# The bias product of a GraphSAGE layer over 128 rows instead of three, in a fused attention and GraphSAGE kernel

## The chip, the core and the metric

The kernel runs on one core of one Trainium2 chip. The metric is device time of one execution in microseconds (us); the table below gives the median of three runs. Times with a decimal point that follow an instruction's name are starts counted from the first instruction of one profiled execution.

## What is computed

The input is a batch of 16 graphs of 1024 nodes with 128 features each, and a weighted adjacency of 1024 x 1024 per graph. Layer 0 is an eight-headed attention that is masked and weighted by the adjacency. Layer 1 first thins the adjacency row by row ("dilation"), and then runs three GraphSAGE steps on the thinned one; in the reference, cut to what matters:

```python
def _sage(x, adj, Wr, Wx, b, mf):
    deg = jnp.clip(jnp.sum(adj, axis=-1, keepdims=True), 1.0, None)
    agg = jnp.einsum('bij,bjd->bid', adj, x) / deg
    out = agg @ Wr + x @ Wx + b
    nrm = jnp.maximum(jnp.linalg.norm(out, axis=-1, keepdims=True), NORM_EPS)
    return out / nrm * mf[..., None]
...
h1 = _bn(jax.nn.relu(_sage(x, adj_d, Wr1, Wx1, b1, mf)), g1, be1)
h2 = _bn(jax.nn.relu(_sage(h1, adj_d, Wr2, Wx2, b2, mf)), g2, be2)
h3 = _bn(jax.nn.relu(_sage(h2, adj_d, Wr3, Wx3, b3, mf)), g3, be3)
xc = jnp.concatenate([h1, h2, h3], axis=-1) * mf[..., None]
return (xc @ Wl + bl) * mf[..., None]
```

The change concerns the `+ b` in `_sage`. `_bn` needs the mean and variance over all graphs, so the three steps can't overlap: each ends in a short stretch in which the statistics are finished before the next begins.

## The kernel before

The program is one long unrolled list of instructions. TensorE (PE), VectorE (DVE) and ScalarE (ACT) run it in the order in which the Python code issues it (`manual_schedule`, L1186); the order was written out by hand, with generators that are advanced at fixed places. SP's queue and GpSimd's queue issue the transfers.

**First part, to about 2414 us.** Attention over all 256 pieces of the adjacency, with the dilation beside it. TensorE works here mostly in parts of its array: 32 rows (score products, L545 and L551) or 32 columns (sums of values, L478 and L483).

**GraphSAGE, from 2414.6 to about 3487 us.** Three steps L = 0, 1, 2, sixteen graphs b, two halves c of 512 nodes: 96 turns in the order L, b, c. A turn is one call of `nodes` (L1081), interleaved with the end of the turn before it and with work for the next graph. On TensorE a turn issues in this order:

- the bias product (`start_with`, L111), which opens the accumulator `own` and lays the bias under all 512 columns. The fp32 bias was cut into three bf16 pieces at the start (`biases`, L90); the product of a 3 x 128 matrix of ones with the 3 x 512 pieces adds them up again, the 128 columns of the piece repeated four times;
- the node's own product x @ Wx into the same accumulator (L1092, four products; every fp32 product is two instructions in the trace, so eight);
- the sums over neighbours `pg` (L1106), four groups of 16 instructions. After the second group comes the transposition `pt` of the **previous** turn's result (L1143, four instructions), except in the first turn of a step. Between the groups stand products for the next graph (`given`, L1077; in step 0 the transposes L1060) and, in the turns of the second half (c = 1) of steps 1 and 2, the output products `py` of the step before (L1033).

On VectorE, once the sums of a turn are complete, there runs in fixed order: scaling and adding (L1124, four), one piece of the next turn's masking (L145, the thinning of the adjacency, four pieces a turn), the row sums of squares (L1132, after ScalarE's L1129), L1134, another piece of L145, L1137, L1138, and L1139, which makes the result `o`. TensorE's `pt` (L1143) reads `o`. In step 0 the degrees (L1117, L1120) come first. Then follow two more pieces of L145 and the statistics L1150. In the turns with c = 1 of steps 1 and 2, VectorE also adds up the output products (L1038).

So turn n's sums release a stretch of VectorE work, and turn n+1's TensorE list waits for the end of it at `pt`, halfway. The bias product of turn n+1 stands between the two.

The bias product is also used in attention, in `value` (L322) and at the end of `conclude` (L413), 32 times each. The constants are made at the very start: `ones3` (L83, L84) by VectorE; `bias3` (L88) is filled by three small transfers on GpSimd's queue (L105).

The adjacency for the turns is fetched by `edges` (L128) on SP's queue, three to four turns ahead.

Of the kernel before, what the change touches and what calls it, by code (L numbers as in the profile page):

```python
# [11 lines left out]
BF = mybir.dt.bfloat16  # L12
# [9 lines left out]
P = 128  # L22
# [12 lines left out]
def swept(ctx: ExitStack, tc: tile.TileContext, t: dict, out: bass.AP, flag: bass.AP):  # L35
# [8 lines left out]
    nc = tc.nc  # L44
    x, adj, nodemask = t["x"], t["adj"], t["nodemask"]
    B, N, D = x.shape
# [6 lines left out]
    const = ctx.enter_context(tc.tile_pool(name="const", bufs=1))  # L53
# [26 lines left out]

        return ap.unsqueeze(2).to_broadcast([P, ap.shape[-1], d])

    ones3 = const.tile([3, P], BF, name="ones3")  # L83
    nc.vector.memset(ones3, 1.0)  # L84


    names = ["L0_gnn_bv", "L0_gnn_bo"] + [f"L1_gnn_b{i + 1}" for i in range(3)]
    bias3 = const.tile([3, len(names), D], BF, name="bias3")  # L88

    def biases():  # L90
        n = len(names)
# [13 lines left out]
            nc.gpsimd.dma_start(bias3[i : i + 1], pieces[i])  # L105
        yield

    def start_with(ps_tile, pieces):

        n = ps_tile.shape[1]  # L110
        nc.tensor.matmul(  # L111
            ps_tile.rearrange("p k d -> p (k d)"), ones3, pieces.unsqueeze(1).to_broadcast([3, n, D]),
            start=True, stop=False,
        )

# [50 lines left out]
    def first_part(p1):  # L166
# [32 lines left out]
        names = ("Wk", "Wv", "Wq", "Wo")  # L199
# [8 lines left out]
        own = one.tile([P, 2], F32, name="own")  # L208
# [75 lines left out]
        def prepare(b):  # L284


            yield False
            xt = xts.pop(b)
            h = shared.tile([P, NB, D], F32, name=f"h_{b}", tag="s", bufs=2)
            hT = shared.tile([P, N], F32, name=f"hT_{b}", tag="s", bufs=2)  # L290

            def turned(c, bank=(ps_m, "m")):
                pt = bank[0].tile([P, 512], F32, name=f"pt_{b}_{c}", tag=bank[1])
                for i in range(HB):
                    nc.tensor.transpose(pt[:, i * P : (i + 1) * P], h[:, c * HB + i, :], ident)
                yield "evict"
                nc.scalar.copy(hT[:, c * HN : (c + 1) * HN], pt[:, :HN])


            kT = pool.tile([P, N], F32, name=f"kT_{b}", tag="kT")  # L300

            def query(c, bank=(ps_m, "m")):
                pq = bank[0].tile([P, 512], F32, name=f"pq_{b}_{c}", tag=bank[1])
                nc.tensor.matmul(pq, wts["Wq"], hT[:, c * HN : (c + 1) * HN], start=True, stop=True)
                yield "evict"
                for g in range(2):
                    nc.scalar.activation(  # L307
                        qTs[c][:, g, :], pq, AF.Identity, bias=bq[:, g : g + 1], scale=own[:, g : g + 1]
                    )

            def key(c, bank=(ps_m, "m")):
                cc = slice(c * HN, (c + 1) * HN)
                pk = bank[0].tile([P, 512], F32, name=f"pk_{b}_{c}", tag=bank[1])
                nc.tensor.matmul(pk, wts["Wk"], hT[:, cc], start=True, stop=True)
                yield "evict"
                nc.scalar.activation(kT[:, cc], pk, AF.Identity, bias=bk)

            v1 = v1s[b % 2]

            def value(c, bank=(ps_m, "m")):  # L320
                pv = bank[0].tile([P, HB, D], F32, name=f"pv_{b}_{c}", tag=bank[1])
                start_with(pv, bias3[:, 0, :])  # L322
                for i in range(HB):
                    n = (c * HB + i) * P
                    nc.tensor.matmul(
                        pv[:, i, :], hT[:, n : n + P], wts["Wv"], start=False, stop=(i == HB - 1)
                    )
                yield "evict"
                nc.scalar.copy(
                    v1[:, c * HB : (c + 1) * HB, :, :HD], pv.rearrange("p k (h d) -> p k h d", d=HD)  # L330
                )

            if b == 0:

                first = layer_norm_relu(h, xt, "a0", 0, HB)
                for _ in range(2):
                    next(first)
                yield "weights"
                yield from first
                yield "weights"  # L340
                yield "biases"
                yield from turned(0)
                yield "turn 1"
                second = layer_norm_relu(h, xt, "a0", HB, NB)
                for _ in range(2):
                    next(second)
                yield from key(0)
                qTs = [pool.tile([P, 2, HN], F32, name=f"qT_{b}_0", tag="qT")]
                yield from query(0, (ps_d, "d"))
                yield from second  # L350
                ready[b] = (xt, qTs, kT, v1)
                yield True
                yield from value(0, (ps_d, "d"))
                yield True
                yield from turned(1)
            else:
                yield from layer_norm_relu(h, xt, f"a{b}")
                for c in range(2):
                    yield True
                    yield from turned(c)  # L360
                for what in (key, value):
                    yield True
                    yield from what(0)

                yield "half 1"
                qTs = [pool.tile([P, 2, HN], F32, name=f"qT_{b}_0", tag="qT")]
                yield True
                yield from query(0)

            ready[b] = (xt, qTs, kT, v1)  # L370
            for what in (key, value):
                yield True
                yield from what(1)
            yield "half 0"
            qTs.append(pool.tile([P, 2, HN], F32, name=f"qT_{b}_1", tag="qT"))
            yield True
            yield from query(1)

        def conclude(b, c, acc, xt):

            yield False
            cx = small.tile([P, HB, H, HD], F32, name=f"cx_{b}_{c}", tag="cx", bufs=1)
            oTs = []
            for g in range(2):
                oT = small.tile([P, HN], F32, name=f"oT_{b}_{c}_{g}", tag="oT", bufs=2)
                nc.scalar.copy(oT, acc[g])
                oTs.append(oT)
            for g in range(2):
                yield True
                on = ps_m.tile([P, HB, 4, 32], F32, name=f"on_{b}_{c}_{g}", tag="m")  # L390
                for i in range(HB):
                    nc.tensor.transpose(
                        on[:, i, :, :].rearrange("p h d -> p (h d)"), oTs[g][:, i * P : (i + 1) * P], ident
                    )
                yield "evict by VectorE"
                rd = small.tile([P, HB, 4], F32, name=f"rd_{b}_{c}_{g}", tag="rd", bufs=2)
                nc.vector.reciprocal(rd.unsqueeze(3), on[:, :, :, HD : HD + 1])
                nc.vector.tensor_tensor(
                    cx[:, :, g::2, :], on[:, :, :, :HD], rd.unsqueeze(3).to_broadcast([P, HB, 4, HD]), ALU.mult
                )  # L400
                nc.gpsimd.tensor_copy(rden[:, 2 * b + c, :, 4 * g : 4 * g + 4], rd)
            yield True
            pc = ps_m.tile([P, 512], F32, name=f"pc_{b}_{c}", tag="m")
            for i in range(HB):
                nc.tensor.transpose(
                    pc[:, i * P : (i + 1) * P], cx[:, i, :, :].rearrange("p h d -> p (h d)"), ident
                )
            yield "evict"
            cxT = small.tile([P, HN], F32, name=f"cxT_{b}_{c}", tag="oT", bufs=2)
            nc.scalar.copy(cxT, pc)  # L410
            yield True
            pr = ps_m.tile([P, HB, D], F32, name=f"pr_{b}_{c}", tag="m")
            start_with(pr, bias3[:, 1, :])  # L413
            for i in range(HB):
                nc.tensor.matmul(
                    pr[:, i, :], cxT[:, i * P : (i + 1) * P], wts["Wo"], start=False, stop=(i == HB - 1)
                )
            yield "evict by VectorE"
            part = xt[:, c * HB : (c + 1) * HB, :]
            nc.vector.tensor_tensor(part, part, pr, ALU.add)  # L420
            if c == 1:
                yield False
                nc.sync.dma_start(x1_d[b], xt)
                yield from layer_norm_relu(xt, xt, f"b{b}")
                nc.sync.dma_start(h0_d[b], xt)
# [655 lines left out]
    def nodes(L, b, c, hT, aT):  # L1081
# [4 lines left out]
        k0 = b * NB + c * HB  # L1086
        width = D + 1 if L == 0 else D
        own = bank(f"own_{L}_{b}_{c}", "o").rearrange("p (k d) -> p k d", d=D)
        start_with(own, bias3[:, 2 + L, :])
        for i in range(HB):  # L1090
            n = (c * HB + i) * P
            nc.tensor.matmul(own[:, i, :], hT[:, n : n + P], wts[f"Wx{L + 1}"], start=False, stop=(i == HB - 1))  # L1092
# [93 lines left out]
    with tc.manual_schedule(  # L1186
# [6 lines left out]
        for L in range(3):  # L1193
# [10 lines left out]
            for b in range(B):  # L1204
# [4 lines left out]
                for c in range(2):  # L1209
                    i = (L * B + b) * 2 + c  # L1210
# [738 lines left out]
```

## Time and profile before

| | us |
|---|---|
| median of 3 runs | 3541.1 (3537.39 to 3546.47) |
| profiled execution, first to last instruction (the only time that the profile gives of it) | 3538.5 |
| TensorE busy (34855 matmuls) | 3433.7, 97% |
| VectorE busy | 3172.6, 90% |
| ScalarE busy | 2289.3, 65% |
| GraphSAGE: bias product of the first turn of steps 0, 1, 2 | 2414.6, 2767.6, 3132.1 |
| a c = 0 turn and the c = 1 turn after it, step 2 | 10.47 and 11.67 |

How to read it: the profile has one row per instruction, with a start and a duration. TensorE's matmuls are pipelined and their ends are modelled, so a row's duration is no measure of what the instruction costs: the distance from one start to the next is. A row such as `PE L1106 MATMUL pg<-y,aT 128*128 128x128 f32 x16` says that 16 instructions used 128 rows and 128 columns of the array and wrote 128 x 128 fp32 each; `3*128` is three rows and 128 columns. `PEld` are the loads of the stationary operand. The bracket at the end of a timeline row is the engine's idle time before it and what ended it.

### The profile page before, as it was taken

What the parts mean: (1) busy time and instruction counts of PE and PEld (TensorE: products, weight loads), DVE (VectorE), ACT (ScalarE), POOL (GpSimd) and SP (SyncE); (2) the same over time, 40 slices, a digit from 0 to 9 for tenths busy, and PEclk for the clock granted to TensorE, in tenths of its full rate; (3) what the DMA queues carried; (4) which work ended last, traced back from release to release, by engine and by line L of the source; (5) the groups of instructions that cost most, each with busy time, mean ns of one, the idle gap of its engine ahead of it and who ended that gap; (6) DMA issues with size and microseconds to landing.
All of it is one profiled execution on the core that took longest, in us unless ns stands there. A gap on an engine that the chain in (4) does not pass through costs nothing. (4 is left out here: it accounts for less than half of the span.)

```text
span 3538.5 us, 86073 instructions
## 1 busy us (share of the span) xinstructions
PE 3433.7 (97%) x34855; PEld 1884.6 (53%) x34855; DVE 3172.6 (90%) x5254; ACT 2289.3 (65%) x3781; POOL 177.6 (5%) x253
## 2 busy tenths in 40 slices
PE   8999999999999999999999999999999899999997
PEld 2333333333333333333333333337999899989997
DVE  7999999999989999999999999997878788878886
ACT  7699689679769869968876885873222333322224
POOL 2000000000000000000000000000000000000000
PEclk9999999999999999999999999999999999999999
DMA  7356456447537636735753873677999799889996
GB/s 233 103 173 195 126 157 195 143 132 221 171 110 216 201 115 198 223 117 163 232 170 118 243 213 108 191 228 263 331 328 331 274 328 331 325 308 333 332 333 217
DMA packets 650121, 772.27 MB, mean 218 GB/s; under 512 B 173264, under 2 KB 569168, under 8 KB 637424
## 3 DMA queue, kind: packets, MB, share of 16 engines
q1 hardware_dynamic: 632672, 708.58, 62.1%
q0 software_dynamic: 15456, 57.30, 4.9%
q8 instruction: 275, 4.51, 0.5%
q14 instruction: 134, 1.10, 0.1%
q10 hardware_dynamic: 1584, 0.79, 0.1%
HBM read 508.50 MB, written 157.29 MB: 188 GB/s over the span
## 5 line engine op out<-in xcount | busy, mean ns | idle before, releaser
L594 DVE TENSOR_TENSOR w<-e,aT 128x1024 f32<-128x1024 f32 x1024 | 1203.7, 1217 | 98.0 <-ACT e L589 97.6
L589 ACT ACTIVATE e<-sc 128x1024 f32<-128x1024 f32 x1024 | 990.8, 1020 | 373.8 <-PE sc L551 369.5
L1106 PE MATMUL pg<-y,aT 128*128 128x128 f32 (+1 forms) x6144 | 737.3, 275 | 0.0
L1106 PEld LDWEIGHTS pg<-y,aT 128*128 128x128 f32 x6144 | 711.8, 192 | 0.0
L478 PE MATMUL acc<-w,v_both 128*32 128x512 f32 x4096 | 676.7, 606 | 10.9 <-DVE w L594 5.7
L483 PE MATMUL acc<-e,eps 128*32 128x512 f32 x4096 | 653.3, 594 | 0.0
L551 PE MATMUL sc<-qT,kT 32*128 32x512 f32 x4096 | 584.0, 640 | 0.3 <-ACT qT L307 0.3
L145 DVE SCALAR_TENSOR_TENSOR aT<-mr,aT 128x1024 f32<-128x1024 bf16 x384 | 458.7, 1216 | 0.0
L483 PEld LDWEIGHTS acc<-e,eps 128*32 128x32 f32 x4096 | 165.5, 110 | 295.0 <-issue 284.9
L1129 ACT ACTIVATE sq<-o 128x512 f32<-128x512 f32 x96 | 60.6, 631 | 361.6 <-DVE o L1124 361.6
L882 DVE TENSOR_TENSOR_SCAN wr<-rk 128x1024 f16<-128x1024 bf16 x128 | 291.6, 2278 | 0.0
L545 PEld LDWEIGHTS <-never 32*32 32x32 bf16 x8192 | 78.2, 87 | 340.1 <-issue 318.5
L545 PE MATMUL sc<-nomask,never 32*32 32x512 bf16 x8192 | 247.0, 385 | 10.8 <-ACT e L589 7.5
L478 PEld LDWEIGHTS acc<-w,v_both 128*32 128x32 f32 x4096 | 106.9, 108 | 241.0 <-DVE w L594 148.9
L551 PEld LDWEIGHTS sc<-qT,kT 32*128 32x128 f32 x4096 | 160.0, 183 | 116.9 <-issue 116.1
L496 PEld LDWEIGHTS pa<-ident,a 128*128 128x128 f32 x1024 | 107.8, 141 | 181.2 <-issue 136.5
L1147 ACT COPY hT<-pt 128x512 f32<-128x512 f32 x96 | 56.3, 586 | 224.2 <-PE pt L1143 214.3
L1124 DVE SCALAR_TENSOR_TENSOR o<-pg,rdeg,mine 128x128 f32<-128x128 f32 x384 | 108.1, 344 | 88.9 <-PE pg L1106 87.1
L895 ACT ACTIVATE wr<-wr,th 128x1024 f16<-128x1024 f16 x128 | 148.0, 1156 | 46.5 <-DVE wr L882 45.6
L496 PE MATMUL pa<-ident,a 128*128 128x128 f32 x1024 | 168.5, 287 | 6.5 <-DMA a<-in_adj 5.8
L503 ACT ACTIVATE nomask<-aT 128x512 bf16<-128x512 f32 x256 | 161.4, 630 | 8.1
L499 ACT COPY aT<-pa 128x512 f32<-128x512 f32 x256 | 151.5, 592 | 12.0 <-PE pa L496 6.2
(225 smaller groups left out, 3927.5 us busy)
## 6 DMA issues: line engine op xcount, KB each, us to landing
aT<-aT_d SPq DMA_DIRECT2D x94, 2048.0 KB, 8.9
mr<-mr_d SPq DMA_DIRECT2D x188, 512.0 KB, 5.8
aT_d<-aT SPq DMA_DIRECT2D x256, 256.0 KB, 4.2
a<-in_adj SPq DMA_DIRECT2D x253, 256.0 KB, 4.2
ad<-in_adj SPq DMA_DIRECT2D x112, 512.0 KB, 4.3
nomask<-nomask SPq DMA_DIRECT2D x512, 96.0 KB, 2.7
nomask<-nomask SPq DMA_DIRECT2D x512, 64.0 KB, 2.6
nomask<-nomask SPq DMA_DIRECT2D x512, 32.0 KB, 2.8
```

Of the source, the lines that this page charges most:

```text
L145: nc.vector.scalar_tensor_tensor(part, mrs[h][:, j : j + 2, :].rearrange("p j n -> p (j n)"), 0.0, part, ALU.is_equal, ALU.mult)
L478: nc.tensor.matmul(acc[g][32 * j : 32 * j + 32, :], v1[:, m, 2 * j + g, :], ws[j // 2][:, j % 2, :], start=(m == 0), stop=False,)
L483: nc.tensor.matmul(acc[g][32 * j : 32 * j + 32, :], eps8, es[j // 2][:, j % 2, :], start=False, stop=(m == NB - 1),)
L496: nc.tensor.transpose(pa[:, k * P : (k + 1) * P], a[:, k, :], ident)
L499: nc.scalar.copy(aT[:, 0, :], pa)
L503: nc.scalar.activation(nomask[:, 0, :], aT[:, 0, :], AF.Relu, bias=1.0, scale=-1e38, accum_out=zeros[:, i : i + 1])
L545: nc.tensor.matmul(scs[j // 2][to : to + 32, j % 2, :], never[rows, rows], nomask[rows, j, :], start=True, stop=False, tile_position=(32 * ...
L551: nc.tensor.matmul(scs[j // 2][:, j % 2, :], kT[rows, mm], qTs[c][rows, g, :], start=False, stop=True, tile_position=(32 * j, 0),)
L589: nc.scalar.activation(e, scs[q], AF.Exp, scale=1.0 / math.sqrt(HD))
L594: nc.vector.tensor_tensor(w, es[q], aT.to_broadcast([P, 2, HN]), ALU.mult)
L882: nc.vector.tensor_tensor_scan(wrs[b], rk(b, 1, N + 1), rk(b, 2, N + 2), -1023.0, ALU.add, ALU.add)
L1106: nc.tensor.matmul(pg[:, i // 2, at : at + width], aT[:, j, i * P : (i + 1) * P], y[:, j, :width], start=(j == 0), stop=(j == NB - 1),)
```

## The change

`ones3` becomes a 128 x 128 matrix of ones, and `bias3` gets 128 rows, of which the last 125 are zero. The bias product of GraphSAGE takes all 128 rows; those of attention take the first three rows of the same tiles, as before. The set of products, their order, their output and the sums that they give are the same. New is one memset of the 128 x 640 bf16 tile on VectorE at the start, which the three transfers into that tile then have to follow.

```diff
-    ones3 = const.tile([3, P], BF, name="ones3")
-    nc.vector.memset(ones3, 1.0)
+    ones_bf = const.tile([P, P], BF, name="ones_bf")
+    nc.vector.memset(ones_bf, 1.0)
...
-    bias3 = const.tile([3, len(names), D], BF, name="bias3")
+    bias3 = const.tile([P, len(names), D], BF, name="bias3")
+    nc.vector.memset(bias3, 0.0)
...
-    def start_with(ps_tile, pieces):
+    def start_with(ps_tile, i, rows=3):
 
         n = ps_tile.shape[1]
         nc.tensor.matmul(
-            ps_tile.rearrange("p k d -> p (k d)"), ones3, pieces.unsqueeze(1).to_broadcast([3, n, D]),
+            ps_tile.rearrange("p k d -> p (k d)"), ones_bf[:rows], bias3[:rows, i, :].unsqueeze(1).to_broadcast([rows, n, D]),
             start=True, stop=False,
         )
...
-                start_with(pv, bias3[:, 0, :])
+                start_with(pv, 0)
...
-            start_with(pr, bias3[:, 1, :])
+            start_with(pr, 1)
...
-        start_with(own, bias3[:, 2 + L, :])
+        start_with(own, 2 + L, P)
```

## The prediction

> **What bounds the kernel now.** I read the page first, then TensorE's timeline over two turns of GraphSAGE, then VectorE's over the same turns, then the waits step by step. From the page: over the span TensorE is the fullest engine, and in GraphSAGE (the last quarter of the slices) the DMA engines are busy too.
>
> ```profile
> PE 3433.7 (97%) x34855; PEld 1884.6 (53%) x34855; DVE 3172.6 (90%) x5254; ACT 2289.3 (65%) x3781; POOL 177.6 (5%) x253
> DMA  7356456447537636735753873677999799889996
> ```
>
> That alone would say: shorten TensorE's list and the time follows. The timeline of TensorE over a c = 0 turn and the c = 1 turn after it (step 2) says otherwise:
>
> ```profile
> 3374.64 0.39 PE L111 MATMUL own<-bias,ones 3*128 3x512 bf16 x1
> 3374.96 1.16 PE L1092 MATMUL own<-weights,h 128*128 128x128 f32 x8
> 3375.95 3.74 PE L1106 MATMUL pg<-y,aT 128*128 128x128 f32 x32
> 3380.08 0.63 PE L1143 MATMUL pt<-ident,o 128*128 128x128 f32 x4 [0.39 <-DVE o L1139]
> ...
> 3383.23 1.95 PE L1106 MATMUL pg<-y,aT 128*128 128x128 f32 x16
> 3385.11 0.38 PE L111 MATMUL own<-bias,ones 3*128 3x512 bf16 x1
> 3385.43 1.16 PE L1092 MATMUL own<-weights,h 128*128 128x128 f32 x8
> 3386.42 1.06 PE L1077 MATMUL pn<-weights,h 128*128 128x128 f32 x8
> ...
> 3391.78 0.60 PE L1143 MATMUL pt<-ident,o 128*128 128x128 f32 x4
> ```
>
> In the first turn TensorE stands before `pt`: 32 instructions of `pg` at 0.112 us end their issue at 3375.95 + 3.58 = 3379.53, and `pt` starts at 3380.08. In the second there is no wait. VectorE shows why; what releases it is the end of the sums before the bias product:
>
> ```profile
> 3374.75 1.12 DVE L1124 SCALAR_TENSOR_TENSOR o<-pg,rdeg,mine 128x128 f32<-128x128 f32 x4 [0.66 <-PE pg L1106]
> 3379.25 0.69 DVE L1139 SCALAR_TENSOR_TENSOR o<-o,f 128x512 f32<-128x512 f32 x1
> ...
> 3389.72 0.69 DVE L1139 SCALAR_TENSOR_TENSOR o<-o,f 128x512 f32<-128x512 f32 x1
> ```
>
> From 3374.75 to 3379.94 VectorE works without a pause, 5.2 us from the end of the old sums to `o`; `pt` follows 0.15 later. Bias product, L1092 and half of the sums are TensorE's share beside it, and in a c = 0 turn of steps 1 and 2 that share is the shorter one. In a c = 1 turn, which also holds `pn` and `py`, `o` is ready at 3390.41 and TensorE gets there at 3391.78: 1.37 us to spare. So c = 0 turns are paced by VectorE up to `pt`, c = 1 turns by TensorE. The waits of TensorE (us in total, times, longest), taken over step 0, step 1 and step 2, agree:
>
> ```profile
> PE pt L1143 <- DVE o L1139: 6.6, 4, 4.7
> ...
> PE pt L1143 <- DVE o L1139: 12.2, 17, 2.5
> ...
> PE pt L1143 <- DVE o L1139: 6.0, 15, 0.4
> ```
>
> Step 0 has only four long ones, but there `pt` is late too, by a gap too short for that list. TensorE's and then VectorE's rows:
>
> ```profile
> 2593.95 0.66 PE L1143 MATMUL pt<-ident,o 128*128 128x128 f32 x4
> 2594.45 1.95 PE L1106 MATMUL pg<-y,aT 128*128 128x129 f32 x16
> ...
> 2588.29 0.16 DVE L1117 TENSOR_SCALAR rdeg<-pg 128x4 f32<-128x4 f32 x1 [1.44 <-PE pg L1106]
> 2593.21 0.69 DVE L1139 SCALAR_TENSOR_TENSOR o<-o,f 128x512 f32<-128x512 f32 x1
> ```
>
> `o` ends at 2593.90 and `pt` starts 0.05 after, its four instructions taking 0.50 to the next row, where an unhindered set (3391.78 to the `pg` at 3392.22) takes 0.44. It holds in both halves: `o` ends 0.05 to 0.07 before `pt` from turn 2 to turn 28. Step 0 is balanced with VectorE just ahead in the say.
>
> [...] the trace has no 128-row bf16 product of 512 columns, but eight bf16 transposes of 128 columns (L889) take 56 ns each, so at most 224 for 512. [...] The trace's loads read 91 ns for the three-row ones and 192 for fp32.
>
> **The change, part by part.** *The product itself.* Before, from starts: a block of 16 `pg` ahead of it takes 1.88 to the bias (3383.23 to 3385.11) where a block followed by an fp32 row takes 1.79 (3392.22 to `py` at 3394.00): 0.09 too much. Bias to L1092: 0.31. L1092 then takes 0.99 (3385.43 to 3386.42) where eight fp32 rows, `pn`, take 0.89 (3386.42 to `pg` at 3387.31): 0.10 too much[...]. After, with one array shape: no excess before, 0.22 for the product with the load of L1092's weights beside it, no excess after. Saved: 0.09 + (0.31 - 0.22) + 0.10 = 0.29, call it **0.30** with the 0.213 that a half-speed stretch suggests for the product (below). That fp32 and bf16 follow one another in one shape without loss is not shown at 128 rows; at 32 rows it is: in attention the bias product (1011.40) follows the last of L551's fp32 rows after 0.41[...] and only its exit, to 128 rows, costs: 0.31 to L415 (1011.71). Bounds: 0.18 [...] (0.09 + 0.09), 0.31 at most; below nothing only by the third rival.
>
> *Where it lies on the path.* The saved time lies between the end of the sums and `pt`.
> - c = 1 turns of step 1: 15 of 16 (the last has no next graph and waits). The margin before `pt`, from the end of L1139 in each to TensorE's arrival, is 1.37, in the last of them 0.48: more than 0.30. 15 x 0.30 = 4.5.
> - c = 1 turns of step 2: all 16, margins 1.37, 0.48 and 0.64 in the last two. 16 x 0.30 = 4.8.
> - The first turn of steps 1 and 2 has no `pt`; after its bias product `pg` follows without a wait. Step 2: 0.30. Step 1 runs at half clock there (bias 2767.58, L1092 2768.11, 0.53 apart, of which 0.427 would be the product, twice 0.213): 0.4.
> - The first turn of step 0 comes from the 32-column shape, so the entry stays: 0.2, and TensorE's list leads from there to the check of the attention (PE to L420 to L973).
> - All c = 0 turns of steps 1 and 2 and all later turns of step 0: **nothing**. TensorE reaches `pt` 0.30 earlier and waits 0.30 longer; in c = 0 turns the idle row grows from 0.39 to about 0.7. Late next is still `o`.
>
> Sum: 4.5 + 4.8 + 0.3 + 0.4 + 0.2 = **10.2 us** of the 28.8 that 96 x 0.30 would be.
>
> *What follows from earlier turns.* A pair of turns in step 2 lasts 22.14, the DMA engines being busy 0.91 of it; at 21.84 it is 0.92, and no wait of TensorE, VectorE or ScalarE in GraphSAGE is for a DMA. In the c = 1 turns VectorE has 0.77 us idle before L1038 and 0.66 before the next L1124, both behind TensorE, so it follows.
>
> *The start.* The new memset has 640 columns; by the fp32 ones (128 columns 0.165, 1024 columns 0.912) it takes 0.6 at most. VectorE is idle for 1.19 us before it casts the identity (2.35), and the memset fits there: nothing; 0.6 if that cover were gone. It is far ahead of the transfers into that tile, which wait for VectorE's pieces until 11.03. The ones tile takes 0.165 for three or for 128 rows. Attention's 64 bias products keep their three rows and cost what they did.
>
> The profiled execution has a span of 3538.5, so 3528.3 after; it lies 2.6 under the median of 3541.1 and within its runs. From the median: 3541.1 - 10.2 = **3531**.
>
> **The rivals.**
> - *Every turn pays.* If the 0.30 were on the path in all 96 turns: 3541.1 - 28.8 = 3512. For it: TensorE is busy 97%. Against it: the rows of `o` and `pt` above, in two turns of three.
> - [...] If the excess comes from the 512-column bf16 product among fp32 ones, or what is won is handed back to the transfers (busy 0.91, so with 0.09 in reserve against a shortening of 0.014), the time stays at 3541. For it: no 128-row pair of this kind in the trace. Against it: the free entry at 32 rows.
> - *Slower.* At 128 rows the ones load like fp32 weights, 0.1 in the open, while both ends stay as they are. Then the path turns lose 0.1 each, 34 x 0.1 = 3.4: 3544.5; c = 0 turns of step 2 have a wait of 0.55 before `pt` that swallows it, step 0 has none, and with its 28 turns it is 3547. It decides from the point where the stretch from last `pg` to second row of L1092 is longer than now (0.21 + 0.31 + 0.21 = 0.73). [...]
>
> **How the numbers follow.** Forecast 0.80, every turn 0.05, no change 0.11, slower 0.04. With 0.18 to 0.31 for the saving the forecast's own times are 3534.7 to 3530.5, and runs spread by some 4 us to either side (3537.4 to 3546.5 before), so 3524 to 3540 holds about eight in ten; it leaves out the first rival and most of the third. About 0.3%, 10.6 us, is what a measurement of this kernel can tell from no change, and 10.2 is just under it: I give faster 0.45 (the forecast on its good side, and the first rival), same 0.52, slower 0.03.
>
> **What would show it.** Right: the bias row reads 128*128 and L1092 starts 0.21 to 0.22 after it, eight L1092 rows take 0.89, c = 1 turns of step 2 last 11.37, c = 0 turns still 10.47 with a longer wait for `o`, and step 0 lasts as long as before. Wrong: c = 0 turns get shorter (first rival), the distances round the bias row stay (second) or grow (third), or a wait for a DMA appears.

## The result, and the profile after

| | before | after |
|---|---|---|
| median (lowest to highest), us | 3540.89 (3537.39 to 3546.47), 8 runs | 3532.36 (3524.36 to 3538.27), 8 runs |
| ratio, with its 95% interval | | 0.9972 (0.9961 to 0.9982) |
| profiled execution, first to last instruction | 3538.5 | 3533.7 |
| c = 0 and c = 1 turn, step 0 | 10.82 and 9.93 | 10.82 and 9.92 |
| c = 0 and c = 1 turn, step 1 | 10.71 and 11.67 | 10.71 and 11.37 |
| c = 0 and c = 1 turn, step 2 | 10.47 and 11.67 | 10.47 and 11.37 |

The turns are medians over turns 2 to 27 of each step (counted from 0), in us from one bias product to the next. The ratio is worth 9.9 us (6.4 to 13.8); 10.2 had been forecast, and 3531 for the time.

The line numbers of the changed kernel, and of those made from it, are one higher than before: the bias product is L112, the node's own product L1093, `pg` L1107, `o` L1140, `pt` L1144.

The page after, in the two lines that were read before:

```profile
PE 3411.2 (97%) x34855; PEld 1887.4 (53%) x34855; DVE 3172.5 (90%) x5255; ACT 2290.3 (65%) x3781; POOL 177.7 (5%) x253
DMA  7356456447537636745753773677999799989996
```

TensorE is busy 22.5 us less, and VectorE has one instruction more, the memset. The span is 4.8 shorter. So most of what TensorE's list lost is not in the span, and these lines don't say where it went. TensorE's timeline over the same two turns of step 2 does (start, duration, instruction, idle time before it):

```profile
3349.13 0.38 PE L112 MATMUL own<-bias,ones_bf 128*128 128x512 bf16 x1
3349.34 1.05 PE L1093 MATMUL own<-weights,h 128*128 128x128 f32 x8
3350.23 3.74 PE L1107 MATMUL pg<-y,aT 128*128 128x128 f32 x32
3354.67 0.63 PE L1144 MATMUL pt<-ident,o 128*128 128x128 f32 x4 [0.70 <-DVE o L1140]
...
3357.81 1.95 PE L1107 MATMUL pg<-y,aT 128*128 128x128 f32 x16
3359.60 0.38 PE L112 MATMUL own<-bias,ones_bf 128*128 128x512 bf16 x1
3359.81 1.05 PE L1093 MATMUL own<-weights,h 128*128 128x128 f32 x8
3360.70 1.06 PE L1078 MATMUL pn<-weights,h 128*128 128x128 f32 x8
...
3366.06 0.60 PE L1144 MATMUL pt<-ident,o 128*128 128x128 f32 x4
...
3370.97 0.38 PE L112 MATMUL own<-bias,ones_bf 128*128 128x512 bf16 x1
```

Three distances have changed: a block of 16 `pg` to the bias is 1.79 (3357.81 to 3359.60), bias to L1093 is 0.21, and eight L1093 rows take 0.89 (3359.81 to 3360.70). The c = 1 turn is 3370.97 - 3359.60 = 11.37. In the c = 0 turn `pt` stands behind an idle 0.70 where it was 0.39, and the turn is 10.47 as before. VectorE over the same turns:

```profile
3349.33 1.12 DVE L1125 SCALAR_TENSOR_TENSOR o<-pg,rdeg,mine 128x128 f32<-128x128 f32 x4 [0.66 <-PE pg L1107]
3353.83 0.69 DVE L1140 SCALAR_TENSOR_TENSOR o<-o,f 128x512 f32<-128x512 f32 x1
...
3364.30 0.69 DVE L1140 SCALAR_TENSOR_TENSOR o<-o,f 128x512 f32<-128x512 f32 x1
```

From the start of L1125 to that of L1140 it is still 4.50: the same list, begun by the same `pg`. TensorE's waits for `o` in steps 0, 1 and 2 (us in total, times, longest):

```profile
PE pt L1144 <- DVE o L1140: 7.2, 4, 4.7
...
PE pt L1144 <- DVE o L1140: 17.0, 17, 2.5
...
PE pt L1144 <- DVE o L1140: 10.4, 15, 0.7
```

Step 1 waits 4.8 more in as many waits, step 2 4.4 more: about 15 times 0.30 in each. That is where the saving of the c = 0 turns went.

### The profile page after: what moved, and what is told of

It reads as the page before. It is cut to its first block, busy times and chain, and to the rows that moved or that the text cites. A ratio compares the mean times of both kernels' runs of the same rounds, so it can differ in the third digit from the quotient of the medians.

```text
span 3533.7 us, 86074 instructions
## 1 busy us (share of the span) xinstructions
PE 3411.2 (97%) x34855; PEld 1887.4 (53%) x34855; DVE 3172.5 (90%) x5255; ACT 2290.3 (65%) x3781; POOL 177.7 (5%) x253
## 5 line engine op out<-in xcount | busy, mean ns | idle before, releaser
L1107 PE MATMUL pg<-y,aT 128*128 128x128 f32 (+1 forms) x6144 | 738.1, 275 | 0.0
L1107 PEld LDWEIGHTS pg<-y,aT 128*128 128x128 f32 x6144 | 712.6, 192 | 0.0
L146 DVE SCALAR_TENSOR_TENSOR aT<-mr,aT 128x1024 f32<-128x1024 bf16 x384 | 458.6, 1216 | 0.0
L1125 DVE SCALAR_TENSOR_TENSOR o<-pg,rdeg,mine 128x128 f32<-128x128 f32 x384 | 108.1, 344 | 90.3 <-PE pg L1107 88.5
```

What stands on the lines that cost most here:

```text
L146: nc.vector.scalar_tensor_tensor(part, mrs[h][:, j : j + 2, :].rearrange("p j n -> p (j n)"), 0.0, part, ALU.is_equal, ALU.mult)
L1107: nc.tensor.matmul(pg[:, i // 2, at : at + width], aT[:, j, i * P : (i + 1) * P], y[:, j, :width], start=(j == 0), stop=(j == NB - 1),)
```

## Experiments

**Only the number of rows (e1).** Step 0 takes 32 rows of the zero-filled tiles, step 1 takes 64, step 2 takes 65; everything else is as in the changed kernel.

```diff
-        start_with(own, 2 + L, P)
+        start_with(own, 2 + L, (32, 64, 65)[L])
```

> The changed kernel with the bias product over 32 rows in step 0, 64 in step 1 and 65 in step 2 (ones and zero rows as before, so the sums are the same). If the shape of the array part is what costs: 32 and 64 rows are parts of the array, and the starts go 0.21 before the product, 0.31 after it and 0.21 after the next row, as with three rows; 65 rows [...] give 0.11, 0.22, 0.11. Turns of the second half: 11.67 in step 1 and 11.37 in step 2. If it is the number of rows that are read or loaded, or the zero rows: something gradual, 64 rows near 65. If it is the change of type: the same in all three steps.

The kernel ran once (3534.86 us), so only its distances and turns are read here. Its timeline in step 1 and then in step 2 (the view ends within the last row of each):

```profile
2900.55 0.39 PE L112 MATMUL own<-bias,ones_bf 64*128 64x512 bf16 x1
2900.87 1.16 PE L1093 MATMUL own<-weights,h 128*128 128x128 f32 x8
2901.86 1.39 PE L1107 MATMUL pg<-y,aT 128*128 128x128 f32 x11
...
3162.23 0.38 PE L112 MATMUL own<-bias,ones_bf 65*128 65x512 bf16 x1
3162.45 1.05 PE L1093 MATMUL own<-weights,h 128*128 128x128 f32 x8
3163.34 0.83 PE L1078 MATMUL pn<-weights,h 128*128 128x128 f32 x6
```

With 64 rows L1093 follows after 0.32 and takes 0.99, as with three rows; with 65 it is 0.22 and 0.89. The c = 1 turns are 11.67 in step 1 and 11.37 in step 2. Step 0 stays at 10.82 and 9.93, as it does with three and with 128 rows, so its turns say nothing; but the distances round its 32-row product do: in medians 0.205 before it, 0.315 after it and 0.213 after the next row, as with three rows. The 64-row product has the same zeros and the same tiles as the 65-row one, so it is neither the data, nor the tile's size, nor the bf16 type among fp32 that cost the 0.30. It goes with the rows of the array that the product takes, and in one jump between 64 and 65.

**What if `o` were never late (e2, e3)?** In the turn loop `pt` is issued after the third group of sums instead of after the second; e2 has the three-row product, e3 the 128-row one.

```diff
-                    if before:
-                        go(before, "transposed")
                     pieces[2]()
                     pieces[3]()
-                    if before:
-                        go(before, "end")
                     go(this, "sums")
+                    if before:
+                        go(before, "transposed", "end")
```

> The kernel before (three rows), with the transposition of the last turn's result, and its statistics, one group of sums later, so that TensorE gets to it 1.79 us later. If VectorE's result is what TensorE waits for in the first-half turns: these lose their wait, 0.55 each in step 2 (15 turns) and 0.80 in step 1 (15), and some 0.06 in 28 turns of step 0: 8.3 + 12 + 1.7 = 22 us, ratio 0.994. If TensorE is the bound throughout (the rival in which every turn pays): no wait is removed, 0 us.

> The changed kernel (128 rows) with the same late transposition. If the change earns 0.30 in a turn wherever TensorE does not wait for VectorE: now in nearly all 96 turns, so 28 us less than the three-row kernel with the late transposition, about 50 less than the kernel before (ratio 0.986); first-half turns of step 2 at 9.6, second-half ones at 11.37. If the transfers take over: a pair of turns in step 2 moves what keeps the DMA engines busy for 20.15 us and would last 20.99, one in step 0 19.5 of 20.0; then waits for a DMA appear before the sums or the masking, and the difference between the two kernels is well under 28.

e2 took 3516.47, ratio to before 0.993 (0.9916 to 0.9944), and e3 3490.01, ratio 0.9851 (0.9835 to 0.9866). The two ratios differ by 0.0079 of 3542, 28 us, and the medians by 26.5, where the same edit was worth 9.9 beside the early `pt`. A c = 0 turn of e3 in step 2, in which TensorE no longer stands before `pt`:

```profile
3206.90 0.38 PE L112 MATMUL own<-bias,ones_bf 128*128 128x512 bf16 x1
...
3208.01 5.52 PE L1107 MATMUL pg<-y,aT 128*128 128x128 f32 x48
3213.37 0.60 PE L1144 MATMUL pt<-ident,o 128*128 128x128 f32 x4
...
3216.49 0.38 PE L112 MATMUL own<-bias,ones_bf 128*128 128x512 bf16 x1
```

The c = 0 turns of e2 and e3 are 9.88 and 9.58 in steps 1 and 2, the c = 1 turns 11.67 and 11.37; in step 0 the c = 0 turns are 10.76 and 10.46, the c = 1 turns 9.88 and 9.585. Turns of every kind lose 0.30. So the 28.8 us of the first rival are there to be had, and the place of `pt` was what withheld two thirds of them. e2 and then e3 over the same 250 us, within step 1 (length; busy time and instructions of PE, PEld, DVE, ACT and POOL; then PE's clock, DMA's share and GB/s):

```profile
2800.00:3050.00 250.00, 250.00 (x2161) 242.03 (x2160) 224.57 (x427) 99.66 (x235) 12.25 (x23) 1.00 0.94 341
...
2800.00:3050.00 250.00, 250.00 (x2221) 249.11 (x2220) 230.42 (x440) 103.48 (x240) 12.76 (x24) 1.00 0.97 353
```

By this view TensorE has no idle time in either, though e3 does 2221 instructions where e2 does 2161: the costs of a change of shape count as busy. A full row of busy time therefore doesn't prove that TensorE paces; step 0 of the kernel before, where `o` was late, has one too (88.00 of 88 us from 2512 on). The weight loads of e3 leave 0.9 of the 250 us, and its DMA engines stand at 0.95 to 0.97 over 250 us of each step.

**Is TensorE still the bound there, or are the transfers (e7)?** e3 without the bias product; the kernel leaves the bias out of the three steps, and L1093 opens the accumulator. **And without the product in the changed kernel (e5)**, the bias left out in the same way.

```diff
-        start_with(own, 2 + L, P)
...
-            nc.tensor.matmul(own[:, i, :], hT[:, n : n + P], wts[f"Wx{L + 1}"], start=False, stop=(i == HB - 1))
+            nc.tensor.matmul(own[:, i, :], hT[:, n : n + P], wts[f"Wx{L + 1}"], start=(i == 0), stop=(i == HB - 1))
```

> The changed kernel without the bias product in GraphSAGE: the bias is left out of the three steps' sums, and the first product by Wx opens the accumulator. If first-half turns and step 0 hide TensorE's share before the transposition altogether, they stay at 10.82 and 9.92 (step 0), 10.71 (step 1) and 10.47 (step 2), and only the second-half turns of steps 1 and 2 shorten, by the product's own 0.216, from 11.37 to 11.15. If some of it is on the path there, they shorten by up to 0.216 as well.

> The changed kernel with the late transposition and without the bias product in GraphSAGE (the bias is left out of the sums). TensorE paces nearly every turn of the kernel with the late transposition, with the transfers busy 0.95 to 0.97. If TensorE goes on to pace: 96 x 0.216 = 21 us less than that kernel, ratio to the kernel before 0.979, all turns 0.216 shorter. If the transfers are next: the share goes to 0.98 or more, waits for a DMA appear, and less than half of the 21 us comes.

e5 ran once (3529.92 us). Its c = 1 turns of steps 1 and 2 are 11.157, 0.213 less, and the medians of all the others stay. e7 took 3471.61, ratio 0.98 (0.9784 to 0.9817), 18 us less than e3 where 21 had been expected; turns of every kind are 0.213 to 0.214 shorter in their medians. No wait of TensorE, VectorE or ScalarE in its steps is for a transfer. Its busiest stretch for the transfers is the one in step 1:

```profile
2800.00:3050.00 250.00, 250.00 (x2244) 250.00 (x2243) 234.52 (x452) 104.52 (x244) 13.30 (x25) 1.00 0.98 358
```

Of the signs that had been named for the transfers, the share of 0.98 came; waits for a DMA and a gain below half did not. So TensorE paces even at a DMA share of 0.98. e5 says the same as the changed kernel in another way: taking the product out altogether pays only in the turns in which the padded one paid.

**Earlier `o` instead of later `pt` (e6).** The second piece of masking (`pieces[1]`, on VectorE) is issued behind the result instead of ahead of it, in the changed kernel; nothing moves on TensorE.

```diff
-                    pieces[1]()
                     if before:
                         go(before, "result")
+                    pieces[1]()
```

> The changed kernel with VectorE's second piece of masking put behind the result instead of ahead of it, TensorE's order as it was. If VectorE's list up to the result paces the first-half turns and step 0: the result comes 0.78 sooner (1.22 for the piece less a wait of 0.27 for ScalarE and the overlap), so first-half turns of step 2 go from 10.47 to about 9.7, of step 1 from 10.71 to 9.93, turns of step 0 from 10.82 and 9.92 to 10.46 and 9.58 (TensorE's own length); together some 33 us less than the changed kernel, ratio to the kernel before 0.988. If it is not VectorE's list: no change. If the later masking holds the next turn's sums: longer turns and waits of L1107 for L146.

e6 took 3507.97, ratio 0.9909 (0.9892 to 0.9925). By the ratios that is 22 us less than the changed kernel, where 33 had been expected. Steps 0 and 2 came out as expected (10.46 and 9.585; 9.71 and 11.37), but the c = 0 turns of step 1 stayed at 10.71. In one of them, VectorE first:

```profile
2913.87 0.17 DVE L1135 TENSOR_SCALAR f<-f 128x4 f32<-128x4 f32 x1
2915.32 0.18 DVE L1138 RECIPROCAL f<-f 128x4 f32<-128x4 f32 x1 [1.27 <-ACT f L1136]
...
2915.73 0.69 DVE L1140 SCALAR_TENSOR_TENSOR o<-o,f 128x512 f32<-128x512 f32 x1
```

and then ScalarE, which it waited for:

```profile
2913.44 0.56 ACT L1098 COPY mine<-own 128x512 f32<-128x512 f32 x1
2913.91 1.28 ACT L1024 ACTIVATE tb<-weights,mf 128x128 f32<-128x128 f32 x4
2915.09 0.20 ACT L1136 ACTIVATE f<-f 128x4 f32<-128x4 f32 x1
```

VectorE's input to L1136 was there at 2914.04, and L1136 began at 2915.09: in between ScalarE made four L1024 (`add_bias`, the output bias), which only the c = 0 turns of step 1 have. VectorE stood idle for about as long as the moved piece takes (1.22 us for one L146).

**ScalarE too (e8).** To e6, the first part of `add_bias` is moved behind L1136.

```diff
                     go(this, "sums")
                     ...
-                    if biased:
-                        next(biased)
                     pieces[0]()
                     if before:
                         go(before, "norm")
                     if before:
                         go(before, "result")
                     pieces[1]()
+                    if biased:
+                        next(biased)
                     beside[1]()
```

> The kernel with the late masking piece, in which step 1's first-half turns did not shorten, and in it ScalarE's first four products for the output bias (L1024, 1.28 us in a row, only in first-half turns of step 1) put behind the square root L1136 of the norm. If ScalarE's square root, waiting behind them, holds the result in step 1: those turns go from 10.71 to about 9.7, as in step 2, 15 us less than the kernel with the late masking piece alone, ratio to the kernel before 0.987. If something else holds step 1 (transfers, or the masking put late): they stay at 10.71.

e8 took 3492.67, ratio 0.9859 (0.9843 to 0.9875), by the ratios 18 us less than e6. Step 1's c = 0 turns are 9.71. ScalarE in such a turn, with L1136 ahead of L1024:

```profile
2923.43 0.56 ACT L1098 COPY mine<-own 128x512 f32<-128x512 f32 x1
2924.06 0.20 ACT L1136 ACTIVATE f<-f 128x4 f32<-128x4 f32 x1
2924.17 0.68 ACT L1024 ACTIVATE tb<-weights,mf 128x128 f32<-128x128 f32 x2
```

TensorE's listed waits for `o` in step 1 fall from seventeen in e6 to two. Waits too short for that list remain: in c = 0 turns of steps 1 and 2 `pt` still starts 0.1 later than the last `pg` would let it, and these turns last 9.71 where e3 has 9.58. e8 and e3 reach about the same by opposite means, earlier `o` and later `pt`; their intervals overlap, so which is faster stays open. Of the kernels that compute the whole, e3 has the lowest median, 52 us below the kernel before.

**The attention's bias products (e4).** They take 128 rows too.

```diff
-                start_with(pv, 0)
+                start_with(pv, 0, P)
...
-            start_with(pr, 1)
+            start_with(pr, 1, P)
```

> The changed kernel with the two bias products of attention over 128 rows too. Entry comes from 32-row score products, so it gains a change of shape (0.41 to about 0.52), the exit loses one (0.31 to 0.22, and the next row from 0.21 to 0.11): 0.1 less for each of 64 products. If TensorE paces attention: 6 us less than the changed kernel (ratio to the kernel before 0.9955). If VectorE or ScalarE does: the same as the changed kernel (0.9972). If the rule were that more rows are better anywhere: 64 x 0.30 = 19 us less.

e4 took 3532.01, ratio 0.9969 (0.9958 to 0.998), not to be told from the changed kernel. The products behind 32-row ones, in the kernel before and then in e4:

```profile
1010.44 1.14 PE L551 MATMUL sc<-qT,kT 32*128 32x512 f32 x8
1011.40 0.38 PE L111 MATMUL pr<-bias,ones 3*128 3x512 bf16 x1
1011.71 1.16 PE L415 MATMUL pr<-attn_w,cxT 128*128 128x128 f32 x8
```

```profile
1009.47 1.14 PE L552 MATMUL sc<-qT,kT 32*128 32x512 f32 x8
1010.54 0.39 PE L112 MATMUL pr<-bias,ones_bf 128*128 128x512 bf16 x1
1010.77 1.05 PE L416 MATMUL pr<-attn_w,cxT 128*128 128x128 f32 x8
```

The change of shape is now ahead of the product instead of behind it. By medians over these products, last score row to bias goes from 0.409 to 0.520, bias to L416 from 0.306 to 0.226, first to second row from 0.213 to 0.109: 0.928 becomes 0.855. That is 0.073 for each of the 56 products that follow 32-row ones. The other eight follow full-array products, and there some 0.28 comes back, as in GraphSAGE. Together this is at most 56 x 0.073 + 8 x 0.28 = 6.3 us, and how much of it is on the path stays open: the two intervals are each some 8 us wide.

## Why the prediction was right, point by point

**The size of one product: right.** Medians of starts in steps 1 and 2: last `pg` to bias 206 ns before and 110 after, bias to L1093 315 and 216, first to second row of L1093 213 and 109. The three differences are 0.096, 0.099 and 0.104, together 0.30. In the prediction the same three terms stand as 0.09, 0.09 and 0.10, which makes 0.28 and not the 0.29 written there; the 0.30 that it went on with was the better figure. e1 shows that 64 rows cost the same 0.30 as three, and 65 nothing. The entry behind 32-row products, which the prediction calls free, is 0.409 from the last score row to the three-row product in the kernel before, and 0.518 to 0.520 to a product of 128 rows (medians to L392, L496 and L825): shown is that the change of shape costs 0.11 there, not that the 0.409 has no excess, which was the author's estimate. How the 0.30 divides can be read in part from the weight loads of the two kernels, before and then after, in the turns shown above:

```profile
3385.11 0.09 PEld L111 LDWEIGHTS <-ones 3*128 3x128 bf16 x1
3385.42 0.97 PEld L1092 LDWEIGHTS own<-weights,h 128*128 128x128 f32 x8 [0.23 <-issue]
...
3359.49 0.10 PEld L112 LDWEIGHTS <-ones_bf 128*128 128x128 bf16 x1
3359.60 1.08 PEld L1093 LDWEIGHTS own<-weights,h 128*128 128x128 f32 x8
```

Before, each of these loads started with its own product: the ones at 3385.11, the weights at 3385.42. After, the ones' load starts 0.11 ahead of its product (3359.60) and the weights' load 0.21 ahead of theirs (3359.81). So in these turns, where the shape changed, nothing was loaded ahead. The 0.10 between the first two rows came where the fp32 load was late. The ones' load that came late costs only about 0.01: it is late as well ahead of the first bias product of step 0 after (load and product at 2416.45), no change follows, and bias to next row is 0.226 there, as in e4's attention, against 0.216. In the attention before, the ones are loaded 0.43 ahead and a change follows, and bias to next row is 0.306, so that an estimated 0.09 (0.306 - 0.216) is left for the change behind the product. That the last 0.10 is the fp32 load is the author's estimate from these starts; no run varies it alone.

**The product itself: right.** 0.213 had been taken. With 128 rows it is 0.216 from its start to the next, and 0.427 in the first turn of step 1 at a clock of 0.50; in e5 and e7 0.213 per turn is what leaving it out saves. The load of the ones reads 97 ns with 128 rows and 91 with three. Where it runs ahead, last `pg` to bias is 0.110, and from one `pg` to the next it is 0.112.

**Which turns pay: right.** c = 1 turns of steps 1 and 2 lost 0.298 to 0.300 each; 30 of them can be read as whole turns, 9.0 us. In the last turn, which ends without a bias product, bias to `pt` went from 4.88 to 4.68. Step 0 and all c = 0 turns of steps 1 and 2 moved by less than 0.01 in their medians. e2 and e3 show the reason by taking it away. In step 0 it was a near thing: with three rows and `o` never late its turns are 10.76 and 9.88 (e2), only 0.06 and 0.04 under what they were. With an earlier `o` the change pays there too: 10.46 and 9.585 in e6.

**Why c = 0 turns don't pay: right for step 2, incomplete for step 1.** "c = 0 turns paced by VectorE up to `pt`" had been read from turns of step 2. The list of VectorE's work before the prediction leaves out that L1137 (L1138 in the changed kernel) waits for ScalarE's square root, L1135 (L1136). In c = 0 turns of step 1 ScalarE's L1024 stands ahead of that root and makes it later than VectorE's own list. In such a turn of the changed kernel, ScalarE and then VectorE:

```profile
2929.40 0.19 ACT L1136 ACTIVATE f<-f 128x4 f32<-128x4 f32 x1
...
2929.63 0.18 DVE L1138 RECIPROCAL f<-f 128x4 f32<-128x4 f32 x1 [0.15 <-ACT f L1136]
```

This is where the 0.24 comes from by which c = 0 turns are longer in step 1 than in step 2 (10.71 and 10.47). So VectorE alone could not have made those turns faster (e6), and both together could (e8). For the change itself it made no difference: `o` is late by either.

**First turns of the steps: about right in steps 0 and 2, half in step 1, and not to be seen in this execution.** 0.9 had been put down for the three. Turn by turn the profiled executions give -0.27 for step 0, +0.79 for step 1 and +0.26 for step 2. What adds to them is TensorE's clock (columns as above, the clock third from the end). In the kernel after, over the `pt` of the second turn and at the starts of steps 1 and 2:

```profile
2439.70:2443.10 3.40, 3.02 (x14) 3.05 (x15) 3.40 (x8) 0.59 (x1) 0.00 (x0) 0.50 0.78 310
2770.20:2774.20 4.00, 4.00 (x19) 3.91 (x18) 0.00 (x0) 2.88 (x7) 0.00 (x0) 0.50 0.47 136
3131.50:3132.60 1.10, 1.10 (x6) 1.01 (x5) 1.10 (x2) 0.86 (x2) 0.53 (x2) 0.50 0.28 112
```

and in the kernel before, at the starts of steps 1 and 2:

```profile
2767.60:2769.50 1.90, 1.90 (x8) 1.46 (x8) 0.00 (x0) 1.30 (x2) 0.00 (x0) 0.51 0.83 254
...
3132.10:3133.20 1.10, 1.10 (x8) 0.85 (x8) 1.10 (x3) 0.96 (x2) 0.47 (x1) 1.00 0.86 354
```

Step 1's first turn has 4.0 us at half clock after and 1.9 before, which is (4.0 - 1.9) / 2 = 1.05 more; less a quarter, it is the 0.79. Step 2's first turn has 1.1 us of it after and none before: 0.55 more, less 0.30, is 0.26. Runs that meet the same clock as the kernel before show it clean: step 2's first turn is 9.15 in e1 (65 rows there) against 9.45, -0.30 as forecast; step 1's is 10.09 in e4 against 10.30, -0.21, half of the 0.4 that had been put down at half clock. The three distances themselves did shrink by 0.41 there (0.354, 0.532 and 0.374 in the kernel before; 0.214, 0.426 and 0.214 in e4). But the first of them lies ahead of the turn, and the clock came back 1.9 us after the bias product in both kernels. In the kernel after, bias to L1093 is 0.427 at a clock of 0.50 and 0.216 at 1.00. Taken from that, what is saved at half clock is worth half once the clock is back: of 0.27 behind the bias product an estimated 0.13, with 0.10 ahead of the next bias product 0.23.

**The sum.** Between the two profiled executions the differences are these. Thirty turns -8.96, turn 0 -0.27, step 0's other turns, the c = 0 turns and the last stretch -0.28; against these, +1.82 from the first part (bias product of turn 0 at 2416.45 against 2414.64; in profiled kernels with the same first part as the kernel after it stands anywhere between 2410.2, e8, and 2418.7, e3), +1.44 in turn 1, where half clock fell on `pt` and the `pg` behind it and not on work ahead of a wait, +0.79 and +0.26 at the starts of steps 1 and 2, and +0.41 in the last turn of step 1 (21.53 to 21.94; 22.85 in e4, whose list there is the same). That is -4.79, the difference of the two spans. The 3528.3 that had been put down for the profiled execution was therefore missed (3533.7). Leaving such positions out, the turns give 8.96 for the thirty, 0.20 for the last turn and 0.27, 0.21 and 0.30 for the first ones, an estimated 9.9 in all. The medians of eight runs have 9.9 as well, but with an interval of 6.4 to 13.8 so close an agreement is in part luck; the turns are the firmer evidence.

**Transfers and start: right.** A pair of turns is 21.84 with a DMA share of 0.93 (0.92 forecast) and no wait of a computing engine for them. The memset of the bias tile took 0.33 and lies in VectorE's idle time ahead of the cast, which fell from 1.19 to 0.84; the cast starts at 2.35 in both.

**The rivals.** "Every turn pays" fails for this kernel and holds with the late `pt` (e2 to e3). The second, that the excess is not the shape's, falls with e1, and its other half, that the transfers take back what is won, with the turns of 11.37. "Slower" needed more than 0.73 from last `pg` to second row of L1093; it is 0.110 + 0.216 + 0.109 = 0.435.

The interval of the ratio, 0.9961 to 0.9982, has 0.997 inside it, so whether the gain is more or less than 0.3% stays open, as the near-even chances for "faster" and "same" had it.

## What to carry to other kernels

Among full-array matmuls, try padding a small one to more than 64 rows with zeros: here the next matmul followed after 0.216 us and not 0.315, and with what a change of shape costs at the two ends 0.30 us was saved for each product. Behind matmuls that themselves take part of the array it was only 0.07 (e4). Before counting instructions, read in each kind of turn what the next wait ends on: the same 0.30 was worth 10 us with `pt` early and 28 with `pt` one group later. And when one engine's list is shortened to free another, look at every engine that feeds the late value, in every stage: in step 1 the work taken off VectorE's path gained nothing until ScalarE's was moved too.

## What the runs showed of the hardware that had not been expected

- The line is sharp: from the bias product to the next it is 0.316 us with 64 rows and 0.220 with 65, and the 0.10 on either side of these is there with 64 rows and gone with 65 (e1).
- Around the bias products, where the shape changed, the load of the next weights started with its own product (L1092 at 3385.42 and 3385.43 in the kernel before); where it did not, ahead of it: by 0.11 for the ones and 0.21 for L1093 in GraphSAGE after, by 0.43 for the ones in attention before.
- TensorE's granted clock was halved (0.50) in blocks that in the kernels before and after lasted 3.41 us each, or 13.65 at the start of step 1, save the last, in which the program ends. The one at the start of step 1 lasted some 10.2 us in e3 and e4 by their clock shares, and it began 8.3 to 11.8 us ahead of the step's first bias product in the kernels before, after and e4. For a difference of 10 us this matters: turn 1 of step 0 was 1.4 us longer after than before.
- TensorE went on pacing over 250 us in which the DMA engines were busy 0.98 of the time (e7). A share this high did not make TensorE, VectorE or ScalarE wait.
